# Grouped quads of a graph layer: sorting the edges' inputs instead of their messages

## The chip, the cores and the metric

One core of one Trainium2 chip. The metric is the device time of one execution, in microseconds (us). Three runs of the kernel before gave 2073.61, 2068.15 and 2074.27 us, median 2073.61. The profiled execution took 2069.4 us, 2067.6 of them inside the profiler's span.

## The reference, cut to what matters

200,000 edges, 6,250 nodes, 128 features. The kernel must compute

```
h    = relu(layernorm(x))                     # 6250 x 128
xw   = h @ W_in
W_e  = (softplus(f_e @ W_f1 + b_f1) - log 2) @ W_f2 + b_f2     # per edge, f_e has 20 numbers
m_e  = xw[dst_e] * W_e * c_e                  # the message of an edge
out  = segment_sum(m_e, src_e, 6250)
y    = x + (softplus(out @ W_o1 + b_o1) - log 2) @ W_o2 + b_o2
```

The edges come sorted by `dst`, so the gather `xw[dst]` of a run of edges touches a narrow window of nodes; `src` is random, so the segment sum is a scatter.

## The kernel before, in words

The edges are cut into chunks of 128, four chunks to a *quad* (512 edges, 391 quads). One pass of a long loop (line 1208) carries every quad through a software pipeline written out by hand: what runs in iteration i at which point ("L", "D0", "PE2", "A0", ...) is put into a table of hooks by `at(...)`, and each engine executes its instructions in that program order.

Every quad goes through the same message part. TensorE makes `z` from the filter inputs (`s1_pe`, L313; the 20 inputs are held as three bfloat16 parts in 123 rows of `ft`), ScalarE makes `a` from it (exp and ln, L318 and L323), TensorE makes `W` (a bias matmul L494 and four fp32 matmuls L505) and gathers the node rows `xg` with a one-hot of `dst` relative to a 21-node window (L497), ScalarE scales `xg` by the edge weight (`xc`, L510), and VectorE multiplies `W` by `xc` (L520): the messages. What becomes of them depends on the kind of quad.

- **Plain** quads (31, at the beginning and the end): equal `src` within a chunk are summed with a comparison matrix `eq` (L357) and a matmul (L532); then GpSimd scatters each chunk with one indirect, accumulating DMA (`scatter`, L582) into one of four accumulators in DRAM. Four scatters a quad.
- **Listed** quads (192): lists made beforehand (`l_eq`, `l_count`, ..., L366 to L444) send repeated nodes to rows of their own, so that the messages are scattered as they stand. Four scatters a quad, and one more per 16 quads for the list.
- **Sorted** (grouped) quads (168, in 21 rounds of 8): no scatter. The nodes are split into 16 groups of 392; every edge gets a slot among 16 x 32 slots by its group and its rank in it, and 64 overflow slots (`rank_group` to `rank_slot`). `perm_oh` (L662) makes the one-hot of slots, `part_rem` (L676) splits the messages into three bfloat16 parts, `permute` (L687) carries the parts into slot order on TensorE (16 matmuls a quad), `perm_out` (L693) copies them to bfloat16, and once in a round four *units* (`unit_oh` L766, `unit_pe` L781 with 96 matmuls, `unit_evac` L792) add the 8 quads' slots into `accT` in SBUF, four groups at a time. The overflow slots of two quads are moved by `over_pe` (12 matmuls, L702 to L704), summed (L718 to L755) and scattered with one scatter.

So the number of scatters is fixed by the kinds: the trace has 768 of listed quads, 123 of plain ones and 96 from overflow slots and lists. `sorted_quads` takes quad 8 and then steps of 2, 2, 2, 3 through the quads. After the loop come a check of flags, the sum of the accumulators and the output matmuls (L1353 to L1446).

The DMAs of the loop are issued by SP in program order: `load_sc` (L288) for a pair of quads brings `ft`, the relative `dst` (`rb`) and the window rows (`wn`); the three bfloat16 parts of the filter inputs are made in blocks of 8 quads (`fb_1` to `fb_4`, L268 to L286) and pass through DRAM (`fsd`). The program issues the scatters as

```
scatter(st[q]["m"][:, c, :P], lst["ji", w][:, 4 * k + c:4 * k + c + 1], l_base(w) + P)   # L803, per chunk
nc.gpsimd.indirect_dma_start(out=accs[k][:rows, :], out_offset=..., in_=s, compute_op=ALU.add)   # L582
```

and the two matmul groups that the change replaces are

```
for c in range(4):                                   # permute, L687; s = 0..3, so 16 a quad
    nc.tensor.matmul(t[:, :PW], mp[q]["pm"][:, c, s * P:(s + 1) * P], high(mp[q]["pt"][:, c:c + 1, :PW])[:, 0], ...)
for c in range(4):                                   # over_pe, L702 to L704; 12 a quad
    nc.tensor.matmul(o[:, :P + 3], w, pt[:, 2 * P:PW], ...)
    nc.tensor.matmul(o[:, :P], w, pt[:, P:2 * P], ...)
    nc.tensor.matmul(o[:, :P], w, pt[:, :P], ...)
```

Of the kernel before, what the change touches and what calls it, by code (L numbers as in the profile page):

```python
# [27 lines left out]
MP0 = 8  # L28
MPGAPS = (2, 2, 2, 3)
MPEND = 0  # L30
RND = 8
EXTRA = 0
RKQ = 8
UOFF = (2, 6)
SW = 16
LEARLY = 8
LLATE = 16
LCAP = 7
PW = 387
MW = 388  # L40
# [7 lines left out]
FPARTS = ((0, 3), (3, 2), (5, 1))  # L48
CQ = 16
EARLY_N = 256  # L50
ZMAX = 60.0
# [3 lines left out]
def tile_gnn(ctx: ExitStack, tc: tile.TileContext, x, fB, cT, srcT, srcr, dstr, win_, wf1, wf2, bias, bo1c, wo1,  # L55
             wo2, consts, ident, cmap, out, n_edges):
# [3 lines left out]
    NB, RB, BE = fB.shape  # L60
    EP = NB * BE
# [3 lines left out]
    NSC = EP // SC  # L65
    HALF = NSC // 2
    spread = big(NSC)
# [6 lines left out]
    caps = base_caps(NP, NSC)  # L74
# [3 lines left out]
    ZL = 3  # L78
    K1_END, K2_END, K3_END = 2, 8, 140
    Z2, Z3 = [0,0,1,1,2,2,3,3,4,4], [5+2*j for j in range(10)]  # L80
    mpq = sorted_quads(NQ)
    mpi = {q: n for n, q in enumerate(mpq)}
    units = unit_its(mpq)
    splain = [q for q in range(NQ) if q not in mpi]
    plain = {q: n for n, q in enumerate(splain)}
    NS = len(splain)
    LB, LE = listed(NS) if spread else (0, 0)
    CE = min(128, EP // P) if spread else EP // P
    CB = min(4 * NS + 64, EP // P) if spread else 0
    lend = splain[LE - 1] if LE else 0  # L90
    scat = [0] * (NQ + 60)
    for q in splain:
        scat[q + (2 if LB <= plain[q] < LE else 4)] += min(4, NCH - 4 * q)
    NW = (LE - LB) // SW
    LR = P * NW
    wend = [splain[LB + SW * (w + 1) - 1] for w in range(NW)]
    for w in range(NW):
        scat[wend[w] + 16] += 1
    for q in mpq[1::2] + mpq[-1:] * (len(mpq) % 2):
        scat[q + 10] += 1  # L100
# [8 lines left out]
    sp_ = edge.enter_context(tc.tile_pool(name="sp", bufs=4))  # L109
# [13 lines left out]
    fmax = cp.tile([P, NB], F32, name="fmax")  # L123
    zcol = cp.tile([P, 4], F32, name="zcol")
    loads = {}
# [3 lines left out]
    x_sb = cp.tile([P, NPT, P], F32, name="x_sb")  # L129
# [10 lines left out]
    accT = cp.tile([P, NP], F32, name="accT")  # L140
    zero = accT[:, :ACC_R // ZR]
    wgtb = cp.tile([P, 1], BF16, name="wgtb")
    iotw = cp.tile([P, GN // 2 + SLOTS], F16, name="iot")
    iot = iotw[:, GN // 2:]
    tri = cp.tile([P, P], BF16, name="tri")
# [3 lines left out]
    ge = cp.tile([P, 4 * RKQ, GRP + 1], BF16, name="ge")  # L149
    dropT = cp.tile([P, EP // P], BF16, name="dropT")  # L150
    mos = []
    for i in range(2):
        mo_ = cp.tile([P, 132], F32, name=f"mo{i}")
        mos.append(mo_)

# [14 lines left out]
    def zero_list(k, j):  # L170
        v = accs[k][ACC_R:].rearrange("(p t) f -> p (t f)", p=P)
        w = LR // ZL
        nc.sync.dma_start(v[:, j * w:(j + 1) * w], zero[:, :w])

    def xt_load(g):
        o, T = groups[g]
        nc.sync.dma_start(x_sb[:, o // P:o // P + T], x[o:o + T * P, :].rearrange("(t p) f -> p t f", p=P))
# [3 lines left out]
    def prep_stat(g):  # L181
# [3 lines left out]
        for t in range(T):  # L185
            nc.vector.bn_stats(bn[:, t], x_sb[:, o // P + t])
# [4 lines left out]
        pst[g] = {"mv": mv, "var": var}  # L191
# [8 lines left out]
    def prep_norm(g):  # L200
# [8 lines left out]
        for t in range(T):  # L209
            nc.vector.tensor_scalar(xn[:, t], x_sb[:, o // P + t], pst[g]["mv"][:, t, 0:1], rs[:, t:t + 1],  # L210
                                    op0=ALU.subtract, op1=ALU.mult)
# [51 lines left out]
    def fb_load(b):  # L263
        t_ = ld.tile([P, FE], F32, tag="fb", name="fb", bufs=2)
        nc.sync.dma_start(t_, fB[b].rearrange("r e -> (r e)").rearrange("(p e) -> p e", p=P))
        fst[b] = {"f": t_}
# [21 lines left out]
    def load_sc(s):  # L288
        n = min(SC, NQ * SEG - s * SC)
        pp, hh, nh = s % HALF, s // HALF, n // SEG  # L290
        top = caps[s]
        ft = fts[s % len(fts)]
        b, o = s * SC // BE, s * SC % BE
# [4 lines left out]
        for j in range(nh):  # L298
            nc.sync.dma_start(rb[j * HB:(j + 1) * HB], reld[s:s + 1, j * SEG:(j + 1) * SEG].to_broadcast([HB, SEG]))
        wn = ld.tile([P, 2, P], BF16, tag="wn", name="wn")  # L300
        _, regs = nc.values_load_multi_w_load_instructions(
            base_i[pp:pp + 1, hh, 0:2 * nh], engines=[SP], min_val=0, max_val=top,
            skip_runtime_bounds_check_because="clamped on the chip to [0, top]")
        for k in range(2 * nh):
            j, c = divmod(k, 2)
            nc.sync.dma_start(wn[j * HB:j * HB + NR, c, :], tab[bass.ds(regs[k] * 3, NR), :])
        loads[s] = (ft, rb, wn)

    def s1_pe(q):
        ft = loads[q // 2][0]  # L310
        j = q % 2
        z = ps.tile([P, 512], F32, tag="A", name="z", bufs=4)
        nc.tensor.matmul(z, ws, ft[:K1, j * SEG:(j + 1) * SEG], start=True, stop=True)  # L313
        st.setdefault(q, {})["z"] = z
# [10 lines left out]
    def s1_oh(q):  # L325
        if q % 2 == 0:
            rb = loads[q // 2][1]
            oh = wk.tile([P, 512], BF16, tag="oh", name="oh")
            v = slice(0, min(2, NQ - q) * HB)
            nc.vector.tensor_scalar(oh[v], rb[v], rowid[v], None, op0=ALU.is_equal)  # L330
            late["oh"] = oh
        st[q]["oh"] = late["oh"]
# [3 lines left out]
    def sb_load(k):  # L336
        qs = splain[2 * k:2 * k + 2]
        t_ = ld.tile([P, 2 * SEG], I16, tag="sb", name="sb", bufs=4)
        for j, q in enumerate(qs):
            if j and q == qs[0] + 1 and q % 2:  # L340
                continue
            n = 2 if j == 0 and len(qs) > 1 and qs[1] == q + 1 and q % 2 == 0 else 1
            o = q % 2 * SEG
            nc.sync.dma_start(t_[:, j * SEG:(j + n) * SEG],
                              src16[q // 2:q // 2 + 1, o:o + n * SEG].to_broadcast([P, n * SEG]))
        sbs[k] = t_

    def plainq(q):
        return q not in mpi and not LB <= plain[q] < LE

    def s1_eq(q):
        if not plainq(q):
            return
        n = plain[q]
        eq = wk.tile([P, 4, P], F32, tag="eq", name="eq", bufs=3)
        v = sbs[n // 2][:, n % 2 * SEG:(n % 2 + 1) * SEG]
        nc.vector.tensor_tensor(eq, v.rearrange("p (c i) -> p c i", c=4),  # L357
                                srcT_sb[:, n * 4:n * 4 + 4].unsqueeze(2).to_broadcast([P, 4, P]), op=ALU.is_equal)
        st[q]["eq"] = eq
# [13 lines left out]
    def l_count(g):  # L373
        t = ps.tile([P, 512], F32, tag="B", name="lcnt", bufs=4)
        for k in range(2):
            eq = lst.pop(("eq", 2 * g + k))
            for c in range(8):
                nc.tensor.matmul(t[:, 8 * k + c:8 * k + c + 1], eq[:, c, :], wgtb, start=True, stop=True)
        lst["cnt", g] = t
# [73 lines left out]
    def l_start(j):  # L453
        mp["L", j] = {"so": idl[:, j:j + 1]}

    def l_dg(j):
        dg = wk.tile([P, P], F32, tag="h", name="ldg", bufs=1)
        nc.scalar.mul(dg, idt, idl[:, j:j + 1])
        mp["L", j]["dg"] = dg

    def l_same(j):
        eq = wk.tile([P, P], F32, tag="rm", name="leq", bufs=1)
        nc.vector.tensor_scalar(eq, mp["L", j].pop("row")[:, :P], idl[:, j:j + 1], None, op0=ALU.is_equal)
        mp["L", j]["eq"] = eq

    def l_sum(j):
        t = ps.tile([P, 512], F32, tag="B", name="lsum", bufs=4)
        for k in range(NACC):
            nc.tensor.matmul(t[:, :P], mp["L", j]["eq"], lst["m", j][:, k], start=(k == 0), stop=(k == NACC - 1))
# [1126 lines left out]
```

## Time and profile before

| | us |
|---|---|
| median of three runs | 2073.61 |
| profiled execution | 2069.4 |
| its span | 2067.6 |
| PE busy (matmul) | 1854.7 |
| DVE busy | 1657.1 |
| POOL busy | 1631.5 |
| ACT busy | 1490.1 |

PE is TensorE, DVE VectorE, ACT ScalarE, POOL GpSimd, SP the engine that issues the plain DMAs. A group of instructions is shown as: line, engine, operation, output<-inputs, shapes, count, then busy time and mean ns of one, then the idle time of the engine just before them and what ended it. "issue" is idle time in which the engine waited for nothing that the profile shows. The busy times of groups add up to more than an engine's busy time, because the records of neighbouring instructions overlap: the DVE groups add up to 1828 us against 1657.1 of busy time. The granted TensorE clock was 0.96 over the span and 0.99 from 400 to 1900 us.

### The profile page before, as it was taken

Reading aid. Unit: us, or ns where it says so; the run is one execution under the profiler, and the core shown is the slowest. Engines: PE = TensorE matmul, PEld = TensorE weight load, DVE = VectorE, ACT = ScalarE, POOL = GpSimd, SP = SyncE. Lnnn points to the kernel's source line nnn. Section 1 sums busy time; section 2 is a strip of 40 time slices with the busy share of each in tenths; the row PEclk is TensorE's granted clock in tenths of the full one; section 3 lists DMA queues with packets and bytes.
Section 4 is the critical chain, followed back from the end, with each engine's and each line's share of the span. In section 5 each row is a group of like instructions: output and inputs, shape, how many; then the busy total and the mean of one; then the engine's idle time right before and its main releaser. Section 6 shows DMA issues by size and latency. Waiting matters only on the chain. (4 is left out here: it accounts for less than half of the span.)

```text
span 2067.6 us, 57535 instructions
## 1 busy us (share of the span) xinstructions
PE 1854.7 (90%) x20381; PEld 1285.7 (62%) x20381; DVE 1657.1 (80%) x4448; ACT 1490.1 (72%) x4083; POOL 1631.5 (79%) x1040
## 2 busy tenths in 40 slices
PE   3489997999999999999999999999999999999956
PEld 2356664666666666666666666666666666677734
DVE  3578896898987888988988978979889787787735
ACT  3368775777776788777778777777778678888714
POOL 3578888888877788887878878888888888888774
PEclk9689998999999999999999999999999999999978
DMA  7887766767766776766667666676676676667648
GB/s 240 227 211 150 125 124 109 128 112 135 130 124 106 126 133 117 136 124 122 121 133 123 122 123 117 118 129 107 129 128 116 112 126 111 110 120 131 129 46 242
DMA packets 381187, 272.56 MB, mean 132 GB/s; under 512 B 97727, under 2 KB 341354, under 8 KB 380898
## 3 DMA queue, kind: packets, MB, share of 16 engines
q0 software_dynamic: 143728, 71.30, 34.9%
q1 hardware_dynamic: 236882, 197.50, 33.8%
q8 instruction: 161, 2.64, 0.5%
q14 instruction: 128, 1.05, 0.2%
q10 hardware_dynamic: 288, 0.07, 0.0%
HBM read 154.45 MB, written 114.24 MB: 130 GB/s over the span
## 5 line engine op out<-in xcount | busy, mean ns | idle before, releaser
L582 POOL DMA_INDIRECT acc<-s,lji x768 | 1237.3, 1611 | 266.9 <-issue 184.6
L687 PE MATMUL pq<-pt,pm 128*128 128x387 bf16 x2688 | 527.9, 339 | 27.0 <-DVE pt L676 10.7
L510 ACT ACTIVATE xc<-xg,cb 128x128 f32<-128x128 f32 x1564 | 446.4, 371 | 121.0 <-PE xg L497 113.8
L505 PE MATMUL W<-w,a 128*128 128x128 f32 x3128 | 464.1, 293 | 0.0
L505 PEld LDWEIGHTS W<-w,a 128*128 128x128 f32 x3128 | 388.7, 196 | 42.0 <-issue 2.6
L781 PE MATMUL un<-so,mst 32*128 32x392 bf16 x8064 | 378.3, 331 | 31.9 <-ACT os L746 19.3
L693 ACT CAST mst<-pq 128x387 bf16<-128x387 f32 x672 | 303.1, 481 | 132.6 <-PE pq L687 130.0
L687 PEld LDWEIGHTS <-pm 128*128 128x128 bf16 x2688 | 259.4, 99 | 211.4 <-issue 16.7
L781 PEld LDWEIGHTS <-mst 32*128 32x128 bf16 x8064 | 228.4, 94 | 175.0 <-issue 70.0
L323 ACT ACTIVATE a<-a,con 128x512 f32<-128x512 f32 x391 | 282.3, 722 | 12.7
L582 POOL DMA_INDIRECT acc<-s,ji x123 | 197.0, 1602 | 82.8 <-issue 25.9
L318 ACT ACTIVATE a<-z 128x512 f32<-128x512 f32 x391 | 237.4, 607 | 33.2 <-PE z L313 17.4
L676 DVE TENSOR_TENSOR pt<-pt 128x512 f32<-128x512 f32 x336 | 231.8, 690 | 5.8
L662 DVE TENSOR_SCALAR pm<-iot,pos 128x576 bf16<-128x576 f16 x672 | 221.4, 390 | 0.0
L520 DVE TENSOR_TENSOR s<-W,xc 128x512 f32<-128x512 f32 x192 | 131.9, 687 | 92.9 <-ACT xc L510 86.0
L792 DVE TENSOR_TENSOR accT<-un,accT 128x392 f32<-128x392 f32 x320 | 158.5, 558 | 58.4 <-PE un L781 58.2
L766 DVE TENSOR_SCALAR so<-iot,mst 128x392 bf16<-128x392 f16 x672 | 191.2, 344 | 5.5 <-PE un L781 5.4
L582 POOL DMA_INDIRECT acc<-os,oji x96 | 155.6, 1621 | 31.1 <-issue 16.2
L497 PE MATMUL xg<-wn,oh 63*128 63x128 bf16 x1564 | 157.2, 222 | 14.5 <-ACT xc L510 8.1
L313 PE MATMUL z<-ft,ws 123*128 123x512 bf16 x391 | 151.6, 388 | 16.1 <-POOL b2rep L927 9.3
L494 PE MATMUL W<-b2rep,onesb 64*128 64x512 bf16 x391 | 153.8, 393 | 0.0
L520 DVE TENSOR_TENSOR pt<-W,xc 128x512 f32<-128x512 f32 x168 | 115.2, 686 | 34.9 <-ACT xc L510 29.4
(209 smaller groups left out, 2431.1 us busy)
## 6 DMA issues: line engine op xcount, KB each, us to landing
rb<-reld SPq DMA_DIRECT2D x391, 64.0 KB
fsd<-f SPq DMA_DIRECT2D x49, 480.0 KB
ft<-fsd SPq DMA_DIRECT2D x195, 120.0 KB
sb<-src SPq DMA_DIRECT2D x169, 128.0 KB
fb<-in_fB_dram SPq DMA_DIRECT2D x49, 320.0 KB
ft<-fsd SPq DMA_DIRECT2D x195, 80.0 KB
wn<-tab SPq DMA_DIRECT2D x782, 15.8 KB
acc<-s,lji POOLq DMA_INDIRECT x768
```

The lines of the kernel that those rows point to most:

```text
L318: nc.scalar.activation(a, st[q]["z"], AF.Exp)
L323: nc.scalar.activation(a, a, AF.Ln, bias=half, scale=0.5)
L505: nc.tensor.matmul(W[:, c, :], st[q]["a"][:, c * P:(c + 1) * P], w2, start=False, stop=(c == 3))
L510: nc.scalar.mul(xc[:, c, :], st[q]["xg"][:, c, :], late["c", q // CQ][:, 4 * (q % CQ) + c:4 * (q % CQ) + c + 1])
L520: nc.vector.tensor_tensor(m[:, :, :P], st[q]["W"], st[q]["xc"], op=ALU.mult)
L582: nc.gpsimd.indirect_dma_start(out=accs[k][:rows, :], out_offset=bass.IndirectOffsetOnAxis(ap=ji, axis=0), in_=s, in_offset=None, compute_ ...
L662: nc.vector.tensor_scalar(pm[:, c], iot[:, :SLOTS], rk[r]["pos"][:, 4 * j + c:4 * j + c + 1], None, op0=ALU.is_equal)
L676: nc.vector.tensor_tensor(pt[:, :, k * P:(k + 1) * P], a, high(a), op=ALU.subtract)
L687: nc.tensor.matmul(t[:, :PW], mp[q]["pm"][:, c, s * P:(s + 1) * P], high(mp[q]["pt"][:, c:c + 1, :PW])[:, 0], start=(c == 0), stop=(c == 3))
L693: nc.scalar.copy(mp[q]["ms", s][:, :PW], mp[q].pop(("q", s))[:, :PW])
L766: nc.vector.tensor_scalar(so, iotw[:, :GN], w[:, 3 * P // 2:3 * P // 2 + 1], None, op0=ALU.is_equal)
L781: nc.tensor.matmul(ts[g][:, :GN], mp[q]["ms", s][v, k * P:(k + 1) * P], mp[q]["oh"][v], start=(q == qs[0] and k == 0), stop=(q == qs[-1] a ...
```

## The change

The loop runs over a list of *items* instead of quads (class `Plan`): S for the quads that are scattered, B for grouped quads, V for an extra quad per round. Quad 12 and then every second quad to quad 378 is grouped (184 quads, 23 rounds of 8); 176 quads are listed, 31 plain; with 23 V items that makes 414 items. What the change does to a grouped quad:

- **Inputs are sorted, not messages.** For a round of 8 quads the filter inputs and the edge weight are loaded in edge order, 128 edges to the partitions (`nat_load`), split into three bfloat16 parts on ACT and DVE (`nat_1` to `nat_4`), and put beside a one-hot of the window (2 x 21 columns, `nat_win`) and the two numbers of the node: 108 columns an edge. `permute` carries these columns into slot order, as rows: 4 matmuls of 512 slots and 4 of the 64 overflow slots a quad, in place of 16 and 12.
- **Messages are made in slot order.** `z` comes from three matmuls with the rows of the three parts, the node rows from 12 matmuls with the sorted one-hot (`edge_win`), the weight and the node of a slot from four small matmuls (`b_ext`). The rest of the message part is as before; the messages stay in fp32 (`bms`).
- **The split in bfloat16 parts moves to the units**: `unit_parts` does it on 8 x 128 columns per unit; `unit_oh`, `unit_pe`, `unit_evac` are as before, now with the strided high halves of fp32 as weights.
- **Overflow slots of 8 quads form item V**: its 512 slots go through the message part and then the path of a plain quad, with `vrow` in place of the loaded `src` row; four scatters a round. `over_pe` to `over_scatter` go.
- The loads of filter inputs and the passes through DRAM (`fb_*`, `fsd`, `ft`, `rb`) are made for the S quads only; `x` is not kept in SBUF, but loaded again for the last addition: 8 of its 13 tiles near the end of the loop, 5 after it.
- Window rows of a grouped quad are loaded by `load_win` (2 loads of 21 nodes a quad). The pool of message buffers `s` has 5 in place of 4 buffers, `pm` has 1 in place of 2.

```diff
-MP0 = 8
-MPGAPS = (2, 2, 2, 3)
+MP0 = 12
+MPGAPS = (2,)
...
+    def load_win(q):
+        wn = wk.tile([P, 3, P], BF16, tag="wb", name="wb", bufs=pl.nwin)
+        for h, reg in enumerate(bases(q)):
+            o = KZ + h * WIN
+            nc.sync.dma_start(wn[o:o + WIN], tab[bass.ds(reg * 3, NR), :].rearrange("(r k) f -> r k f", k=3))
...
+    def rows3(z, ft):
+        for k, n in enumerate(ZROWS):
+            yield nc.tensor.matmul(z, wsb[:n, k], ft[:n], start=(k == 0), stop=(k == 2))
+
+    def edge_win(xg, ft, wn, c, k):
+        nc.tensor.matmul(xg[:, c, :], ft[KZ:KX, c * P:(c + 1) * P], wn[KZ:KX, k, :], start=(k == 0), stop=(k == 2))
...
+            cs = [(c, k) for c in range(4) for k in range(3)]
+            for j, _ in enumerate(rows3(z, ft)):
+                for c, k in cs[4 * j:4 * j + 4]:
+                    edge_win(xg, ft, bq[q]["wn"], c, k)
...
+        elif kind == "V":
+            for j, e in enumerate(pl.rounds[q]):
+                o = j % 2 * OVC
+                for k in range(3):
+                    nc.tensor.matmul(xg[o:o + OVC, j // 2, :], vq[q]["f"][KZ:KX, j * OVC:(j + 1) * OVC],
+                                     bq[e]["wn"][KZ:KX, k, :], start=(k == 0), stop=(k == 2))
...
+    def nat_load(r):
...
+            nc.sync.dma_start(fn[:, v] if n > 1 else fn[:, j], cols(fN, 4 * KN, q, d, n))
+            nc.sync.dma_start(dn[:, v] if n > 1 else dn[:, j], cols(dstT, 4, q, d, n))
+            for k in range(2):
+                nc.sync.dma_start(bn_[:, k, v] if n > 1 else bn_[:, k, j],
+                                  cols(base0[k:k + 1].to_broadcast([P, base0.shape[1]]), 2, q, d, n))
...
-    def permute(q, s):
-        t = ps.tile([P, 512], F32, tag="B", name="pq", bufs=4)
-        for c in range(4):
-            nc.tensor.matmul(t[:, :PW], mp[q]["pm"][:, c, s * P:(s + 1) * P], high(mp[q]["pt"][:, c:c + 1, :PW])[:, 0],
-                             start=(c == 0), stop=(c == 3))
+    def permute(q):
...
+        for c in range(4):
+            w = sts[r % 2][:, 4 * j + c, :]
+            nc.tensor.matmul(f[:KS], w, pm[:, c, :GRP * CAP], start=(c == 0), stop=(c == 3))
+            nc.tensor.matmul(o[:KS, :OVC], w, pm[:, c, GRP * CAP:], start=(c == 0), stop=(c == 3))
...
+    def slot_ext(t, f):
+        for c in range(4):
+            nc.tensor.matmul(t[:, 3 * c:3 * c + 3], f[:KS, c * P:(c + 1) * P], selb[:KS], start=True, stop=True)
...
+    def unit_parts(r, s):
+        m = bms[r % 2][:, :, s]
+        rm = wk.tile([P, RND, P], F32, tag="rem", name="rem", bufs=1)
+        nc.vector.tensor_tensor(rm, m, high(m), op=ALU.subtract)
+        lo = wk.tile([P, RND, P], BF16, tag="low", name="low", bufs=1)
+        nc.vector.tensor_tensor(lo, rm, high(rm), op=ALU.subtract)
...
+            at(max(0, i - 3), "L", nat_load, r)
...
+                at(max(0, u - WLEAD + 4), "L", load_win, q)
+                at(u - 1, "D2", perm_oh, q)
+                at(u, "PE2", permute, q)
+                at(u + 1, "A0", perm_out, q)
+                at(pl.ext[q], "PE2", b_ext, q)
+                at(pl.ext[q] + 1, "D0", b_ext_copy, q)
+                at(p, "A0", b_copy, p)
```

Here `u` is the item in which a grouped quad is sorted, at most 7 items before its own place `p`, and `i` the item in which its round is ranked.

1102 lines of the change are left out of this document (610 added, 492 removed).

## The prediction

> **What bounds the kernel now.** I read the busy times first. PE is busiest, so it looks like the bound; three engines lie close behind.
>
> ```profile
> PE 1854.7 (90%) x20381; PEld 1285.7 (62%) x20381; DVE 1657.1 (80%) x4448; ACT 1490.1 (72%) x4083; POOL 1631.5 (79%) x1040
> ```
>
> Then the costliest groups. Three of them are one instruction, the scatter: 768 + 123 + 96 = 987 on POOL.
>
> ```profile
> L582 POOL DMA_INDIRECT acc<-s,lji x768 | 1237.3, 1611 | 266.9 <-issue 184.6
> L582 POOL DMA_INDIRECT acc<-s,ji x123 | 197.0, 1602 | 82.8 <-issue 25.9
> L582 POOL DMA_INDIRECT acc<-os,oji x96 | 155.6, 1621 | 31.1 <-issue 16.2
> ```
>
> Third, POOL's timeline in the middle of the run. The columns are start, duration, engine, line; the bracket is the idle time before.
>
> ```profile
> 1000.56 1.54 POOL L582 DMA_INDIRECT acc<-s,lji  x1 [0.30 <-issue]
> 1002.40 1.54 POOL L582 DMA_INDIRECT acc<-s,lji  x1 [0.30 <-issue]
> 1004.25 1.56 POOL L582 DMA_INDIRECT acc<-s,lji  x1 [0.31 <-issue]
> ```
>
> The reader is to see that 0.30 us follow every scatter although nothing is waited for: "79% busy" is a full engine. A scatter costs 1589.9/987 = 1.611 us plus 0.306 (226.7 us of "issue" before 742 of them), 1.917 in all. The table by stretches gives the middle:
>
> ```profile
> 400.00:1900.00 1500.00, 1429.70 (x16202) 985.08 (x16201) 1272.82 (x3442) 1155.26 (x3181) 1236.17 (x766) 0.99 0.69 122
> ```
>
> The columns after the stretch are the busy times of PE, PEld, DVE, ACT and POOL, then the clock, the DMA share and GB/s. POOL made 766 scatters in 1500 us, 1.958 each: 98% of its full rate. PE was busy 95%, DVE 85%. At the end POOL runs alone, with PE at 1.2 of 12 us from 1996 to 2008; its last scatter is
>
> ```profile
> 2006.32 1.54 POOL L582 DMA_INDIRECT acc<-os,oji  x1 [0.30 <-issue]
> ```
>
> So **POOL's queue of scatters is the bound**, with PE level beside it. The execution as a sum: first scatter at 55.2; 987 x 1.917 = 1892; POOL waits for others 60; 59.7 from the last scatter's end (2007.9) to 2067.6. The run itself is 1.8 us longer than the span (2069.4), and the median of the runs is 1.002 times that.
>
> **The change part by part, POOL.** Listed quads fall from 192 to 176 and plain ones stay at 31; a round still sends four overflow scatters (before one per two quads, now item V), and there are 23 rounds for 21. The instruction lists show 704 + 215 + 11 = 930 scatters, 57 fewer: 57 x 1.917 = **-109 us**. Two memsets of 3456 columns join POOL's start; by the 32x1024 row (946 ns) they take 6.4 us, beside 9.8 us in which POOL waited for `b2p`. I count 3 us (0 to 6.4). After the loop 1.09 MB of `x` are loaded again; from 2015 us the tail moved 242 GB/s at a DMA share of 0.89, so +4.5 us (0 if the loads hide).
>
> **PE.** Marginal prices come from starts in PE's timeline, since the records overlap:
>
> ```profile
> 1003.67 1.56 PE L687 MATMUL pq<-pt,pm 128*128 128x387 bf16 x8
> 1005.16 0.25 PE L702 MATMUL po<-pt,pm 128*64 128x131 bf16 x1
> 1005.99 0.39 PE L494 MATMUL W<-b2rep,onesb 64*128 64x512 bf16 x1
> 1006.32 1.16 PE L505 MATMUL W<-w,a 128*128 128x128 f32 x8
> 1007.31 0.38 PE L313 MATMUL z<-ft,ws 123*128 123x512 bf16 x1
> 1007.62 4.16 PE L781 MATMUL un<-so,mst 32*128 32x392 bf16 x96
> 1011.72 0.39 PE L494 MATMUL W<-b2rep,onesb 64*128 64x512 bf16 x1
> ```
>
> Eight `pq` take 1.49 (0.187 each), twelve `po` 0.83, a bias matmul with four `xg` 0.33, W 0.99 to 1.09, a unit 4.10. Removed: 168 quads x (16 x 0.187 + 0.83) = 642; overflow sums 84 x 0.58 (`orow` 0.30, `osum` 0.28) = 49; per grouped quad the 123-row `z` (0.22) and the `xg` (0.11), 61. Added: `permute`, four times a 512-column matmul (0.22, the `z` row) and a 64-column one (0.06, the `po` spacing), 184 x 1.12 = 206; `z` and windows, three 512-column matmuls each beside four of 128 on other rows. The nearest row is bias beside `xg`, 0.33, so 184 x 0.99 = 182 (0.66 if fully concurrent, 1.3 if not: 121 to 239). `b_ext` by `lcnt` (16 in 0.40): 21. Eight more units 33. Per V item 0.66 + 0.22 + 24 x 0.06 + 1.09 + 1.4 (eight fp32 records and the four weight sums) + 0.3 = 5.1, x 23 = 117. The weight column of plain quads as its own matmul: 15. Net 574 - 752 = -178: PE 1855 -> **about 1677** (1616 to 1734).
>
> **DVE.** Removed: `part_rem` 231.8; overflow instructions 59.5; 23 of 49 input blocks at 2.45, 56; 92 `oh` at 0.36, 33; 8 `eql` 10; together 390. Added: `unit_parts` 184 x 1.22, the 128x1024 `eql` row, 224, so that the split costs nearly what it did; 64 more `pm` and `so` 39; 32 evacuations 16; 23 message products 16; 184 small PSUM copies at 0.22 (the `ldup` row) 41; `nat_*` 23 x 4.2 (three passes priced by the 128x640 rows, 0.82; two one-hots at most the 512 row, 0.68; two small ones) 97; V 30; two rounds of ranking 10. Sum 473. Net +83; the groups add up to 1828 for 1657 busy, so x 0.906 = +75: DVE 1657 -> **about 1732**. ACT loses 519 us by the rows (303 of `mst`, 183 of `pt` columns and overflow work, 33 of input blocks) and gains about 268 (154 for sorted columns, 57 for 23 items, 57 other); it ends near 1240 and binds nothing.
>
> **DMA and SP.** Each round adds 128 x 8 x 4 = 4096 packets, some of 8 and 16 bytes, 94,000 in all; about 50,000 go (`ft`, `rb`, `wn`, `fsd`, `fb`). The plain queue spends 0.338 x 16 x 2067.6 / 236,882 = 47 ns a packet, so the share of 0.69 rises by some 0.04 (by 0.1 if a tiny packet costs twice that). SP issues fewer DMAs but reads bases 391 times instead of 196; a pair's window loads start about 1.1 us after its other loads in the trace, so +0.2 ms of SP time, in a queue whose longest wait (278 us behind `f`, L284) falls by half. I cost both at nothing; what hides them is the lead of the loads, below.
>
> **The sum.** 2067.6 - 109 + 3 + 4.5 = 1966 span, with POOL's 60 us of waits kept. That is the choice: DVE has less spare, but `s` has five buffers and PE is 10% lighter. Plus 1.8, times 1.002: **1972**. If the 60 us vanish 1912; if scatters also ran at 1.54, 1846.
>
> A rule that speaks against it: scatters of 1.54 us in the quiet end average 1.61 in the run. The Trainium skill ("SBUF — State Buffer", "SBUF: two separate sides") says that VectorE's two-port instructions lock GpSimd out of a shared port pair, so that it cannot write descriptors. The trace agrees in the direction, but no row ties a long scatter to one DVE instruction; by the rule the sum would be that of the second rival.
>
> **Rivals.**
> - *DVE takes over.* Needed in the middle: 23 rounds of 36.5 scatters at 1.917 are 70 us each, and DVE's share of a round is about 66 (1732, less an estimated 210 of work at both ends, by 23). Its waits speak for it:
>
> ```profile
> DVE s L520 <- ACT xc L510: 86.0, 85, 4.2
> DVE accT L792 <- PE un L781: 58.2, 54, 5.3
> DVE ojd L751 <- ACT os L746: 49.5, 21, 13.7
> ```
>
> The third goes with the overflow path; the second stays; of all `xc` waits (132) I keep half. 1732 + idle at the start 33, from 60 to 200 us 40, from 1960 on 58, + 58 + 66 = 1987, so 1993. With `pm` single, `perm_oh` waits for `permute` where two quads are sorted in consecutive items (45 times, at most 2 us): up to 2083.
> - *Scatters stretch.* The 0.07 us above 1.54 grows with DVE's busy share (80% to 88%): 930 x 0.007 = 7 us, 1979.
> - *Late loads, slower than before.* Place: `nat_load` in SP's queue. Its 4096 packets fill each of 16 engines for 12 us at 47 ns, 24 at twice that. `load_pair` behind it is issued three items before use, some 13.5 us. At 24 us it comes about 14.6 us late (4 of its own included); with one quad buffered for POOL (7.7) the starved rest is 6.9 x 23 rounds = 159: 2131. It is slower than before from about 4.4 us of starvation a round. Against it: PE waited 6.0 us for `ft` in the whole run, and the burst shares the engines with little else.
> - *POOL better fed* than now, below 1940.
> - That overflow falls into the slow repair loop I exclude: counted on the reference's inputs, a quad overflows by at most 57 of its 64 slots.
>
> **How the numbers follow.** 1972 as the bound stays POOL: 0.50 (1940 to 1995). DVE 0.25 (1993 to 2060, a tenth of it beyond). Stretch 0.05. Late loads 0.11. Better fed 0.09. The range from 1925 to 2060 leaves out half of the last and nearly all of the slow cases. Faster by over 0.3%, about what a measurement of this kernel tells from none: 0.86; within it 0.03; slower 0.11.
>
> **What would show it.** Right: 930 scatters with 0.30 us before nearly each, PE near 1680, DVE near 1730, a last scatter near 1903 and 64 us behind it. DVE as bound: POOL's idle before scatters released by DVE `s`, DVE over 92% in the middle. Late loads: PE `z` or `xg` waiting for DMA `ft`, `wn` or `wb` once per 17 items. Wrong altogether if strided weights slow the units (4.10 us) or the scatter's price moves.

## The result, and the profile after

The changed kernel takes 2409.73 us (median of 4 runs, 2405.53 to 2415.01) where the kernel before takes 2072.39 beside it (2068.15 to 2074.27): a ratio of **1.163, interval 1.160 to 1.167**. The forecast was 1972 us with a range to 2060. It is wrong in sign and lies 438 us too low. The profiled execution took 2406.4 us, with a span of 2404.6.

The busy times of the changed kernel:

```profile
PE 1975.6 (82%) x21648; PEld 1389.7 (58%) x21648; DVE 1717.5 (71%) x4480; ACT 1257.1 (52%) x3311; POOL 1583.2 (66%) x988
```

DVE (1732 forecast) and ACT (1240) came out as worked out. PE should have been 1677. Every share is lower than before, while the run is longer. The scatters in the groups of the changed kernel (count, busy, mean ns, idle time before them and what ended it):

```profile
L672 POOL DMA_INDIRECT acc<-s,lji x704 | 1166.5, 1657 | 498.7 <-DVE s L604 174.0 <-issue 165.3 <-DMA acc<-s,lji 91.4
L672 POOL DMA_INDIRECT acc<-s,ji x215 | 350.0, 1628 | 258.2 <-ACT ji L653 160.0 <-issue 48.3 <-DMA acc<-s,ji 40.2
L672 POOL DMA_INDIRECT acc<-os,oji x11 | 17.3, 1577 | 5.1 <-ACT oji L541 2.4 <-ACT a L362 1.5 <-issue 0.9
```

The count is the 930 of the forecast and the price nearly so (1.649 us in the mean, 1.611 before). But POOL now waits for others: 762 us of idle before scatters, of which "issue" is only 214. Its timeline at the place shown of before, and its last scatter:

```profile
1003.39 1.81 POOL L672 DMA_INDIRECT acc<-s,ji  x1 [8.16 <-ACT r L208]
1005.50 1.54 POOL L672 DMA_INDIRECT acc<-s,ji  x1 [0.30 <-issue]
...
2336.00 1.54 POOL L672 DMA_INDIRECT acc<-s,ji  x1 [0.30 <-issue]
```

The first scatter starts at 75.5 us (55.2 before), the last one ends at 2337.5. With 930 x 1.917 taken off, the time between them leaves 479 us in which POOL waits for others, where the prediction kept 60. The 67 us behind the last scatter are near the 64 of the forecast.

The table by stretches of the changed kernel (PE, PEld, DVE, ACT, POOL, then granted clock, DMA share and GB/s):

```profile
400.00:1900.00 1500.00, 1283.60 (x14748) 885.19 (x14747) 1141.55 (x3027) 820.57 (x2175) 989.30 (x597) 0.89 0.49 81
```

In the same 1500 us the kernel before made 766 scatters with PE 1429.70, at a clock of 0.99 and a DMA share of 0.69. Now it makes 597, one each 2.51 us, PE is busy 86% at a clock of 0.89, and the DMA engines have *less* to do. What the clock is about shows in PE's timeline:

```profile
1007.95 0.19 PE L809 MATMUL po<-pm,st 128*108 128x64 bf16 x1
1009.01 0.63 PE L536 MATMUL lrw<-ldg,onesf 128*128 128x128 f32 x2 [0.87 <-ACT xc L594]
1009.57 0.60 PE L560 MATMUL W<-b2rep,onesb 64*128 64x512 bf16 x1
...
1010.11 2.07 PE L577 MATMUL W<-w,a 128*128 128x128 f32 x8
...
1012.85 1.14 PE L518 MATMUL lsum<-lm,leq 128*128 128x128 f32 x8
...
1014.35 1.16 PE L577 MATMUL W<-w,a 128*128 128x128 f32 x8
```

After a stop of 0.87 us eight fp32 matmuls take 2.07 us. At 1012.85 eight of the same shape take 1.14 again, and so do the next ones of this line (1.16). The granted clock of the single microseconds from 1009 to 1013 is 0.61, 0.50, 0.50 and 0.68, so it was half for about 3.4 us. A PE that has waited works more slowly for some microseconds here, and its "busy" time grows without more work.

To separate the two, I weighted PE's busy time with the granted clock in steps of 2 us. Before: 1854.7 us busy are 1811 at full clock, with 213 us of idle beside them. After: 1975.6 are 1747, with 428 idle. The 337 us between the spans are therefore **-64 of work, +185 of slow clock, +215 of idle time**.

What ended the idle times of DVE and of PE in the changed kernel (us in all, times, longest):

```profile
DVE s L604 <- ACT xc L586: 180.6, 126, 11.3
DVE accT L893 <- PE un L882: 116.5, 57, 5.1
DVE eql L418 <- DMA sb<-src: 100.9, 12, 13.6
```

```profile
PE xg L565 <- DVE oh L378: 84.8, 51, 4.0
PE be L823 <- DVE ex L832: 43.0, 4, 12.3
PE po L809 <- DVE ex L832: 33.6, 9, 5.0
```

DVE waits for loads, for ACT and for PE; PE waits for small things that DVE owes (a one-hot, a copy of 12 columns). Two places show how. First, a round's loads, in SP's timeline:

```profile
438.48 0.41 SPq L687 DMA_DIRECT2D fn<-in_fN_dram  x1
438.94 0.57 SPq L688 DMA_DIRECT2D dn<-in_dstT_dram  x1
439.56 1.95 SPq L690 DMA_DIRECT2D bn<-in_base_dram  x2
441.55 10.62 SPq L388 DMA_DIRECT2D sb<-src  x4
```

`nat_load` issues 4096 packets of 8 to 336 bytes. Behind it four `sb` issues take 10.62 us; the median of one is 0.43. Everything stops for it, DVE first, then PE:

```profile
456.96 1.22 DVE L418 TENSOR_TENSOR eql<-sb,srcT_sb 128x1024 bf16<-128x1024 int16 x1 [13.57 <-DMA sb<-src]
```

```profile
459.01 0.77 PE L536 MATMUL lrw<-ldg,onesf 128*128 128x128 f32 x2 [14.10 <-DVE ex L832]
```

Such stops come about a round apart: DVE waits 8 to 14 us for `sb` at 257, 358, 457, 1110, 1210 and 1314 us, and about 3 us at 733, 826 and 919. Second, DVE's order, in its timeline and in PE's:

```profile
1016.36 0.85 DVE L698 TENSOR_REDUCE fmax<-fn 128x1 f32<-128x672 f32 x1
1017.12 1.22 DVE L860 TENSOR_TENSOR rem<-bm 128x1024 f32<-128x1024 f32 x1
1018.37 1.23 DVE L862 TENSOR_TENSOR low<-rem 128x1024 bf16<-128x1024 f32 x1
1019.52 1.01 DVE L869 TENSOR_SCALAR so<-iot,ex 128x392 bf16<-128x392 f16 x4
1020.44 0.16 DVE L832 COPY ex<-be 128x12 f32<-128x12 f32 x1
```

```profile
1017.18 0.38 PE L808 MATMUL pf<-pm,st 128*108 128x512 bf16 x1
1020.65 0.21 PE L809 MATMUL po<-pm,st 128*108 128x64 bf16 x1 [3.09 <-DVE ex L832]
```

PE wants a PSUM bank for `po`. By the order of the program the bank is free when DVE has copied the 12 columns of `be`, and that copy of 0.16 us stands at the head of the next item, behind all that DVE has to do for this one: ranking, splitting, one-hots.

### The profile page after: what moved, and what is told of

It reads as the page before. It is cut to its first block, busy times and chain, and to the rows that moved or that the text cites. A ratio compares the mean times of both kernels' runs of the same rounds, so it can differ in the third digit from the quotient of the medians.

```text
span 2404.6 us, 58531 instructions
## 1 busy us (share of the span) xinstructions
PE 1975.6 (82%) x21648; PEld 1389.7 (58%) x21648; DVE 1717.5 (71%) x4480; ACT 1257.1 (52%) x3311; POOL 1583.2 (66%) x988
## 3 DMA queue, kind: packets, MB, share of 16 engines
q1 hardware_dynamic: 283038, 153.25, 24.1%
## 5 line engine op out<-in xcount | busy, mean ns | idle before, releaser
L672 POOL DMA_INDIRECT acc<-s,ji x215 | 350.0, 1628 | 258.2 <-ACT ji L653 160.0
L882 PE MATMUL un<-so,bm 32*128 32x392 bf16 x2944 | 342.8, 359 | 12.4 <-DVE ldup L434 5.6
L882 PE MATMUL un<-so,rem 32*128 32x392 bf16 x2944 | 330.1, 357 | 0.0
L882 PE MATMUL un<-so,low 32*128 32x392 bf16 x2944 | 326.1, 352 | 0.0
L586 ACT ACTIVATE xc<-xg,cb 128x128 f32<-128x128 f32 x828 | 239.5, 386 | 95.3 <-PE xg L565 44.2
L808 PE MATMUL pf<-pm,st 128*108 128x512 bf16 x736 | 244.2, 423 | 6.4 <-ACT s L627 3.9
L594 ACT ACTIVATE xc<-xgb,ex 128x128 f32<-128x128 f32 x736 | 207.3, 363 | 0.0
L869 DVE TENSOR_SCALAR so<-iot,ex 128x392 bf16<-128x392 f16 x736 | 193.7, 325 | 0.0
L339 PE MATMUL xgb<-wb,bfe 42*128 42x128 bf16 x2208 | 190.5, 221 | 3.5 <-DVE accT L893 3.5
L336 PE MATMUL z<-bfe,wsb 64*128 64x512 bf16 x552 | 178.4, 392 | 0.2
```

What stands on the lines that cost most here:

```text
L336: yield nc.tensor.matmul(z, wsb[:n, k], ft[:n], start=(k == 0), stop=(k == 2))
L339: nc.tensor.matmul(xg[:, c, :], ft[KZ:KX, c * P:(c + 1) * P], wn[KZ:KX, k, :], start=(k == 0), stop=(k == 2))
L586: nc.scalar.mul(xc[:, c, :], st[n]["xg"][:, c, :], v)
L594: nc.scalar.mul(xc[:, c, :], xg[:, c, :], bq[q]["ex"][:, c, 0:1])
L808: nc.tensor.matmul(f[:KS], w, pm[:, c, :GRP * CAP], start=(c == 0), stop=(c == 3))
L869: nc.vector.tensor_scalar(so, iotw[:, :GN], bq[q]["ex"][:, s, 1:2], None, op0=ALU.is_equal)
```

## The experiments

Four theories were tried. **A**: late loads (`nat_load`), the prediction's slower rival. **B**: hand-overs between PE and DVE, through banks and through the order on DVE. **C**: DVE's amount of work. **D**: PE's own work. Beside them stands the prediction's first step: POOL's queue as the bound of the kernel before. All ratios are to the kernel before, run on the same chip as the experiment. Differences between ratios are given in us of its median, 2072. Runs without an interval were single runs; the others have two or more.

### Round loads packed (e1)

```diff
-        for j, dj, q, d, n in runs(pl.rounds[r]):
-            ... fn, dn, bn_ from columns of fN, dstT, base0 (strided by quad)
+        nc.sync.dma_start(fn, fR[:, RND * 4 * KN * r:RND * 4 * KN * (r + 1)])
+        nc.sync.dma_start(dn, dstT[:, RND * 4 * r:RND * 4 * (r + 1)])
+        nc.sync.dma_start(bn_, base0[r:r + 1].to_broadcast([P, 4 * RND]))
```

> The changed kernel with the loads of a round (node-ordered features, target indices, window bases) laid out by rounds, so that one round is 3 DMAs of 128 packets instead of 4 DMAs of 7168 small ones; the same work otherwise. Theory A (late loads: the small packets hold SP's queue, and four sb issues behind them took 10.6 us at 441.6 instead of 1.7): DVE's waits for sb fall from 101 to under 25 us, the four or five PE pauses of 12 to 14 us a hundred us apart go, and the time falls by 100 to 170 us, to about 2240 to 2310. Theory B (the lock-step through the PSUM banks and DVE's order makes the loss; loads only show up where there is slack): under 40 us, 2370 to 2410. If it is all late loads, as the prediction's slower rival had it, the time comes down to about 1990.

Measured: 2337.3 us, ratio 1.120 (1.118 to 1.123), **89 us faster** than the changed kernel; clock 0.885. (The 7168 in the text above is a slip: the packets fell by 3728 a round, so there were about 4096.) DVE's wait before `eql`:

```profile
DVE eql L418 <- DMA sb<-src: 14.2, 6, 7.7
```

SP's timeline now shows four `sb` issues right behind the round's loads at their usual price:

```profile
325.79 1.86 SPq L388 DMA_DIRECT2D sb<-src  x4
```

Theory A's waits went as it said, from 101 to 14 us; the gain of 89 us is about as large as they were and lies a little below its range of 100 to 170. Four fifths of the 438 us over the forecast stay.

### The two small edits for the banks, each alone (e2, e3)

```diff
-        nc.vector.tensor_copy(ex..., bq[q].pop("te")[:, :12])      # b_ext_copy, at ext + 1, "D0"
+        nc.scalar.copy(ex..., bq[q].pop("te")[:, :12])             # e2: at ext + 1, "A0"
```

```diff
-            xg = ps.tile([P, 4, P], F32, tag="B", name="xgb", bufs=4)
+            xg = ps.tile([P, 4, P], F32, tag="A", name="xgb", bufs=4)   # e3
```

> The changed kernel with the small copy of `be` (128x12) made by ScalarE one item after its matmul instead of VectorE. Theory B (PE waits for the bank that this copy frees, and it stands in DVE's queue behind the long work of the item before): the PE waits be, po, rkp and lrw released by DVE ex (122 us in all) go nearly to zero, the clock rises, and the time falls by 60 to 150 us. Theory A (late loads): those waits were only the echo of DVE being held by sb; 0 to 40 us. Theory C (DVE itself is late, whatever it frees): the waits come back under another name (oh, accT, G), the time moves by less than 30 us.

> The changed kernel with the four sums of windows (`xgb`) in the other group of four PSUM banks, that of z, xg and W, so that the group B holds one bank less. Theory B (too few banks in group B): waits released by ACT xc L594 (lcnt, rkp, lpre: about 30 us) go, POOL's and ACT's idle falls, 40 to 120 us faster. Theory A and C: within 25 us of the changed kernel; or a few tens slower, where z now waits for a bank of group A.

Measured, one run each: e2 2430.7 us, ratio 1.164, nothing gained; e3 2401.3, ratio 1.150, 28 us. In e2 PE's waits for `ex` on DVE are gone, and others took their place:

```profile
PE lcnt L428 <- ACT xc L594: 45.1, 10, 6.6
PE W L560 <- DVE bm L604: 43.7, 4, 14.3
```

The second has the length of a stop for `sb`. It seems that as long as DVE is held by loads, it does not matter which of its debts PE runs into. Taken alone this spoke for A and C against B.

### The kernel before without 192 scatters (e4)

```diff
             for c in range(nchunks(q)):
+                if c == 3:
+                    sc_n[0] += 1
+                    continue
                 scatter(st[q]["m"][:, c, :P], ...)                  # listed quads
```

> The kernel before, with the fourth of the four scatters of each listed quad left out (192 of 987; those edges' sums are missing from the output). The prediction's first step says that POOL's queue is the bound: POOL then needs 795 x 1.917 = 1524 us, and PE, level beside it, is left as the bound: the time falls to where PE is busy throughout, about 1970 to 2010. If POOL was not the bound but PE (95% busy, 99% from 1700 to 1900): within 20 us of the kernel before, 2050 to 2075.

Measured, one run: 2054.2 us, ratio 0.983, 34 us. POOL had 192 x 1.917 = 368 us less to do.

```profile
400.00:1900.00 1500.00, 1426.40 (x16231) 984.59 (x16231) 1268.43 (x3448) 1153.11 (x3191) 982.75 (x602) 1.00 0.61 115
```

PE, DVE and ACT do in these 1500 us what they did before (1429.70, 1272.82, 1155.26); POOL is at 66% instead of 82%, and the pace is nearly the same (about 1% higher by the ratio, because this chip runs the kernel before in 2089 us). The 34 us are a little more than the 20 that the second expectation allowed, and far from the 1970 to 2010 of the first. **POOL's queue was full, but it was not the bound.**

### The order of `oh`, DVE's amount, PE's amount, POOL's amount (e5 to e8, all on e1)

```diff
-            if i < NI:
-                s1_oh(i)
+            if i + 1 < NI:
+                s1_oh(i + 1)                                        # e5
```

```diff
-        ... rm and lo: two passes of 128x1024 over the messages     # e6, unit_parts
-        un[r, s] = (high(m), high(rm), lo), []
+        un[r, s] = (high(m),) * 3, []
```

```diff
-            for k in range(3):                                      # e7, unit_pe
+            for k in range(2):
```

In e6 the units add the first part three times in place of the three parts, so PE's work stays. e8 has e4's edit in the changed kernel.

> The kernel with packed round loads (e1, 1.120 of before) and with the one-hot `oh` of a plain or listed quad's targets made one item earlier, ahead of VectorE's other work of the item. Same work. Theory B2 (what is left is the lock-step: PE stops 53 times, 100 us, for `oh`, which stands behind the long stretch of VectorE's item before; each stop lowers the granted clock): these waits go below 30 us, the clock rises from 0.885, 50 to 120 us faster, ratio 1.06 to 1.10. Theory C (VectorE is late whatever it hands over): the waits come back at the next thing that it owes, s or bm, G, pm or ex; less than 30 us, ratio 1.105 to 1.125.

> The kernel with packed round loads (e1) and without the split of the collected messages into three parts: the two passes of `unit_parts` are left out, 184 of 1.22 us (224 us of VectorE's 1714), and the units read the first part three times, so the sums of grouped quads keep only the first of three parts. PE, ACT, POOL and the loads are unchanged. Theory C (VectorE's in-order queue is what PE waits for): 80 to 200 us faster, the clock above 0.92, ratio 1.03 to 1.08. Theory D (PE's own work at the granted clock is the bound, and VectorE has room): less than 30 us.

> The kernel with packed round loads (e1) and with two of the three parts in the units' matmuls (64 instead of 96 in each of 92 units; the third part is still computed and not added). PE loses 92 x 32 matmuls: by the 4.10 us of a unit 126 us at full clock. Theory D (PE is the bound): 110 to 160 us faster, ratio 1.045 to 1.07. Theory C (VectorE's order and the waits between the engines set the pace): under 60 us, ratio above 1.09, and PE's idle time grows by the rest.

> The kernel with packed round loads (e1) and without the fourth scatter of each listed quad (176 of 930; those edges' sums are missing from the output). The prediction's step (the sum is POOL's queue) would give 176 x 1.917 = 337 us less. Theories B, C and D: POOL is no bound, under 30 us; if the shorter queue frees message buffers earlier, up to 50.

| run | taken away | time, us | ratio (interval) | against e1 |
|---|---|---|---|---|
| e5 | nothing, `oh` one item earlier | 2260.8 | 1.089 (1.085 to 1.093) | -65 |
| e6 | 224 us of DVE | 2135.7 | 1.029 (1.026 to 1.032) | -190 |
| e7 | 126 us of PE | 2234.6 | 1.077 (1.071 to 1.082) | -91 |
| e8 | 337 us of POOL | 2321.3 | 1.118 (1.115 to 1.122) | -4 |

POOL counts for nothing. Of the time that the removed instructions cost, 0.85 comes back on DVE and 0.72 on PE. Counted by what the engines' busy time lost, it is nearly all: 199 us of DVE (1714 to 1515), and 95 us of PE at full clock (1755 to 1660, weighted as above). Two engines that worked side by side would not both give so much; I read it as their taking turns. In e5, with the same work, the waits that it was made for are gone. PE's row in e1, then in e5:

```profile
PE xg L565 <- DVE oh L378: 99.9, 53, 4.2
PE xg L565 <- DVE oh L378: 1.7, 1, 1.7
```

So a part is order (B2, the order of DVE's work). e6 fits C, but in it this row falls to 15.1 us too: the cut takes work from in front of `oh`, so that its 190 us hold some of what e5 gains by order alone. e7 lies between the forecasts of C and D in time, and PE's idle time did not grow (374.5 us in e1, 374.0 in e7), which speaks against C's reading of it.

### More hand-overs moved (e9, e10), and more work for PE (e11)

e9 is e5 with the edits of e2 and e3. e10 adds

```diff
-            at(k - 2, "D2", unit_parts, r, s)
+            at(k - 3 if r + 1 < len(pl.rounds) else k - 2, "D2", unit_parts, r, s)
```

and e11 is e5 with

```diff
-        nc.tensor.matmul(W..., onesb[b:b + HB], b2rep[b:b + HB]..., start=True, stop=False)
+        for h in range(3 + 1):
+            nc.tensor.matmul(W..., onesb[b:b + HB], b2rep[b:b + HB]..., start=True, stop=(h < 3))
```

> The kernel with packed round loads and the early `oh` (e5, 1.089 of before) and with both of the edits that were tried alone and gave 0 and 28 us: the small copy of `be` on ScalarE, `xgb` in the other group of banks. Same work. Theory B (each hand-over between PE and VectorE that is taken out gives its waits back once the larger ones are gone): the waits by ex (rkp 30, po 25, un 20) and by xc L594 go, 40 to 90 us faster, ratio 1.045 to 1.07. Theory C (VectorE is late by its amount of work): under 20 us.

> As e9, and the split of the messages (`unit_parts`, 2.44 us of VectorE ahead of each unit) one item earlier, so that an item's stretch of VectorE work at a unit is shorter by a third. The amount is the same. Theory B2 (bursts, not the amount, make VectorE late): another 20 to 60 us off e9. Theory C (the amount): within 15 us of e9.

> The kernel e5 (packed loads, early `oh`) with the bias matmul of W made four times instead of once for each of 414 items: 1242 more matmuls of 512 columns, by 0.22 us each 273 us of PE's time at full clock, output unchanged. Theory D (PE's own work is the bound): 200 to 280 us slower, ratio 1.185 to 1.225. Theory B (PE spends some 12% of its time stopped and some more at the half clock that follows a stop; the extra work is done partly in that time and keeps the clock up): 60 to 150 us slower, the clock rises above 0.93.

Measured: e9 2224.1 us, ratio 1.071 (1.065 to 1.078), 37 us less than e5, a little under what B expected. The two edits gave 0 and 28 us alone; with these intervals 37 cannot be told from their sum, so it isn't shown that they act more strongly together. e10 2185.0, ratio 1.053 (1.047 to 1.058), another 39 us without a change of amount. e11 2405.1, ratio 1.159 (1.152 to 1.165), 144 us *more* than e5 for 1242 more matmuls. Weighted with the clock PE's work is 1996 us in e11 against 1762 in e5, so 234 more (runs with the same matmuls spread from 1747 to 1764). Some 0.6 of each microsecond of PE is paid: more than nothing, and less than by a bound. The clock rose only from 0.909 to 0.920, so the filler did not buy it back.

### Where the ranking stands (e14, e18), and DVE's amount once more (e17, on e10)

```diff
-        self.rank = [self.perm[qs[0]] - 7 for qs in self.rounds]
+        self.rank = [self.perm[qs[0]] - 12 for qs in self.rounds]   # e14; 15 in e18
```

> As e10 (1.053 of before), and a round's ranking and its input split (rank_group, nat_max, nat_2, nat_4, nat_win, rank_own, rank_slot: about 10 us of VectorE over six items) five items earlier, so that it no longer falls on the item of the round's first unit. In e10 PE waited 28 us before units for `pr` and VectorE had up to 8 us of work in one item there; summed over the plan the work above 5.3 us in an item falls from 152 to 100 us. Theory B2 (bursts): 20 to 50 us faster, ratio 1.03 to 1.045. Theory C (amount): within 12 us of e10.

> As e14, but the ranking of a round begins eight items earlier than in e10 instead of five, so that both of its banks are free two items before the round's first unit. The work above 5.3 us in an item is 103 us by the plan (e14 100, e10 152). Theory B2 (order): the waits of PE before units for `pr` and `rt` (28 us in e10, 66 in e14) go, 40 to 80 us faster than e10 with the clock's part, ratio 1.015 to 1.035. Theory C (amount): within 12 us of e10 and e14, 1.045 to 1.055.

> As e10 (1.053 of before), without the split of the messages (the same cut as in e6: 224 us of VectorE, one part of three summed). In e1 that cut gave 190 us when VectorE's hand-overs were still late. Theory C (VectorE's amount still sets the pace with PE): 80 to 140 us, ratio 0.985 to 1.015. Theory B (the hand-overs that e5, e9 and e10 moved were what the cut had relieved): under 50 us, ratio above 1.03, and PE above 95% busy in the middle.

Measured: e14 2185.6 us, ratio 1.048 (1.043 to 1.054), and e18 2170.3, ratio 1.046 (1.044 to 1.049): 9 and 13 us by the ratios, and e14's interval overlaps that of e10. e17 2105.0, ratio 1.012 (1.010 to 1.015), 83 us for 224 us of DVE. PE's largest wait of this kind in e10, e14 and e18:

```profile
PE un L878 <- DVE pr L758: 28.2, 10, 4.0
```

```profile
PE un L878 <- DVE rt L782: 65.6, 21, 4.7
```

```profile
PE un L878 <- DVE ldup L434: 71.0, 22, 4.7
```

I read this as one wait under three names. A unit needs all four banks of its group, so it waits for whatever DVE frees last, and moving one debt away brings up the next. Theory C's expectation holds for e14 and e18 (within 12 us, or nearly), and e17's 83 us lie at the lower end of its range; the split's microsecond on DVE is worth 0.37 now instead of 0.85.

### What held the kernel before (e12, e13, e15, e16)

e12 has e7's edit in the kernel before (115 us of PE), e13 that and e4's. e15 leaves `part_rem` out, e16 has all three cuts.

```diff
     def part_rem(q, k):
         ...
-        nc.vector.tensor_tensor(pt[:, :, k * P:(k + 1) * P], a, high(a), op=ALU.subtract)
```

> The kernel before with two of the three parts in the units' matmuls (64 instead of 96 in each of 84 units): 2688 fewer matmuls, 84 x 1.37 = 115 us of PE by the 4.10 us of a unit. POOL, VectorE, ScalarE and the loads as before. If PE was the bound of the kernel before, as the run without 192 scatters suggests: 80 to 115 us faster, ratio 0.945 to 0.96. If POOL was, as the prediction's first step has it: under 20 us. If both stood level: about 30.

> The kernel before with both cuts: without the fourth scatter of each listed quad (192 of 987) and with two of three parts in the units (115 us of PE). Alone they gave 34 and 25 us. If POOL and PE stood level and each covered the other: more than the sum of both, 100 to 140 us, ratio 0.93 to 0.95. If neither was the bound, but the order between the engines (a third engine, VectorE at 85% in the middle): about the sum or less, 40 to 65 us, ratio 0.97 to 0.98, with the clock lower again.

> The kernel before without its split of the messages (`part_rem`, 336 of 0.690 us, 232 us of VectorE's 1657): the second and third parts are zeros that were written once, so the sums of sorted quads keep one part of three. PE, ACT, POOL and loads unchanged. If VectorE was the bound: 100 us or more, ratio under 0.955. If PE, POOL and VectorE stood level, each covering the others: 15 to 40 us, ratio 0.98 to 0.993, with POOL at 98% of its rate from 400 to 1900 us again. If VectorE had room: under 10 us.

> The kernel before with all three cuts: 192 scatters, a third of the units' matmuls and `part_rem` left out. The first two together gave 75 us (0.964). If VectorE was the third level engine: another 60 to 120 us, ratio 0.905 to 0.935. If it had room: 0.955 to 0.965.

| run | taken away | time, us | ratio (interval) | gain, us |
|---|---|---|---|---|
| e4 | 368 us of POOL | 2054.2 | 0.983 | 34 |
| e12 | 115 us of PE | 2051.0 | 0.988 (0.983 to 0.993) | 25 |
| e15 | 232 us of DVE | 2046.8 | 0.985 (0.980 to 0.990) | 32 |
| e13 | POOL and PE | 2009.9 | 0.964 (0.958 to 0.970) | 75 |
| e16 | all three | 1966.0 | 0.946 (0.943 to 0.948) | 113 |

e4 is a single run, and the intervals of e12 and e15 reach some 10 us to either side. The first two alone make 59, all three alone 91; together they make 75 and 113, which with these intervals is hardly more than the sums. So none of the three was the bound. Of what is taken away from one engine alone 9% (POOL), 22% (PE) and 14% (DVE) comes back. e12 and e15 alone came out as engines that stand level would have it (about 30; 15 to 40). The joint cuts gave less than such engines should: e13's 75 lies between its two expectations (40 to 65, 100 to 140), and so do e16's 38 us for its third cut.

In e12 the stretch from 400 to 1900 us reads

```profile
400.00:1900.00 1500.00, 1384.03 (x14203) 944.27 (x14201) 1285.31 (x3486) 1172.24 (x3230) 1254.26 (x775) 0.97 0.70 124
```

775 scatters instead of 766: POOL, at 99% of its rate, lets little more through, and PE, with less to do, stands still more and loses clock (0.99 to 0.97). Relieving one engine runs into the others. Whether it is their amounts or the order between them isn't settled for the kernel before.

## Why the prediction was wrong, point by point

- **The failed step: "So POOL's queue of scatters is the bound, with PE level beside it"**, and the sum built on it, with 57 x 1.917 = 109 us taken off at full price and "POOL's 60 us of waits kept". The reading of POOL was right (0.30 us after every scatter, 98% of its rate). The conclusion was not: a queue that is full need not set the pace if others are nearly full too. By e4 a microsecond of POOL was worth 0.09, so I estimate 10 us for the 57 scatters. And the waits were not kept: by the prediction's own count they are 479 us in place of 60. e8 shows the same in the changed kernel: 176 scatters fewer gave 4 us.
- **What set the pace** in its place, beside the late loads (89 us), was PE and DVE waiting for each other. The forecast costed each engine by its sum of work and let them run beside each other. In the changed kernel they take turns (0.85 and 0.72 in e6 and e7): earlier hand-overs with the same work gave 153 us in all (e5 to e18). Each turn leaves a gap on PE, and slow clock follows the gaps. Between the two spans lie 337 us: 215 more of idle PE and 185 of slow clock, against 64 of work saved. The prediction had no term for either.
- **"PE 1855 -> about 1677"** was mis-sized: -64 us at full clock, not -178. From starts in PE's timeline, weighted with the clock, summed over the run: `z` and windows of grouped quads 217 us (182 forecast; 1.18 a quad, between 0.99 and the upper bound of 1.3), `permute` 219 (206), and bias matmuls with `xg`, without the `xg` of item V, 151. The last were 130 before and I let them fall by 20: the bias matmul had been hidden beside its quad's `xg` (0.33 for both), and a grouped quad has none at that place any more, so it costs 0.32 alone. These three are +35, +13 and +41, 89 of the missing 114. The units were right: 385.7/92 = 4.19 us, 362.6/84 = 4.32 before, so strided weights cost nothing.
- **DVE 1732, ACT 1240, 930 scatters** were right (1717, 1257, 930), and useless without the order. The rival "DVE takes over" named the right engine, but not how: its sign was DVE over 92% in the middle, and DVE is at 76%. It added DVE's busy time and half of its own waits; what PE loses by waiting for DVE was not in it, and 2083 was its end. `pm` with one buffer cost DVE 25 us, against at most 90.
- **"Scatters stretch"** had the sign right and the size too small: 1.611 to 1.649 us a scatter, 0.038 where it expected 0.007, some 35 us of POOL's time, which by e8 cost next to nothing.
- **"Late loads"** was right in place (`nat_load`, 4096 packets, once per round) and too large in size (159 us worked out, 89 measured), and got 0.11. It named the wrong victim, `load_pair` behind it; what came late was `sb`, which SP issued late. The price was wrong as well: a packet of the plain queue took 33 ns in the mean (0.241 x 16 x 2404.6 / 283,038), not 47.
- **"I cost both at nothing"** for DMA share and SP: the share fell (0.69 to 0.49) where it was to rise by 0.04, and SP's part was not free, as e1 shows.

Against the kernel before the loss is 16.3% of its time. Packed loads give back 4.3, the earlier `oh` 3.1, `ex` and `xgb` together 1.8, the earlier `unit_parts` 1.9, the ranking 0.6; **4.6 stay** in e18, the fastest version with all of the work. No version with the whole computation beats the kernel before. Leaving the split out still gives 83 us for 224 of DVE (e17). That cut takes away amount and, with it, the stretch of work ahead of each unit, and no run separates the two. Whether another order of the same work could give the rest back isn't settled, since each move so far brought up the next wait. That the stops cause the slow clock is a reading of the timeline; no run changed the clock by itself.

An estimate of what the idea could give at best: PE's 1747 us at full clock with the overhead of the kernel before (2067.6/1811 = 1.142) are 1995, 3.5% less than before.

## What to carry to other kernels

An engine that is full in the profile is a candidate for the bound, and one cheap cut of its work shows whether it is one. Here, with three engines at 85 to 98%, a cut on one of them was worth a tenth to a fifth of its price. In the changed kernel, where none is full, a cut on PE or DVE was worth 0.7 to 0.85 of it. When a change rewrites the order of work, cost the hand-overs and not only the sums: for each small result that another engine needs, ask what stands ahead of it in its engine's queue, and which bank it holds meanwhile. Many small descriptors held up the queue that issues them, so lay data out by use before it is loaded.

## What the runs showed of the hardware

- **Issuing can stall behind earlier small packets.** Four `sb` issues took 10.62 us behind `nat_load`, and meanwhile the 16 DMA engines had little to do on average (a mean does not show whether one of them was full). The table by stretches of the changed kernel has a DMA share of 0.11, and 5 GB/s, for five of these microseconds:

```profile
445.00:450.00 5.00, 0.00 (x0) 0.00 (x0) 0.00 (x0) 1.96 (x6) 2.59 (x2) 0.60 0.11 5
```

  From 443 to 449 us the trace has 635 packets, all of 8 bytes, about 105 a microsecond. By their size they are the window bases (`bn`), the smallest packets of the round's loads. e1 packed all three kinds of loads at once and doesn't separate them. With 384 packets a round instead of 4096, four such issues took 1.86 us. The Trainium skill ("DMA: Bandwidth & Descriptors", "Issuing engines are not separate DMA queues") calls the sequencer's time to start a DMA usually small; here it was 10.62 us ahead of a wait of 13.57.
- **Half clock followed a stop of under a microsecond.** After 0.87 us of idle the granted clock was half from 1009.2 to 1012.6. The Trainium skill ("TensorE: Matmul & The Clock Gate", "What's actually happening") gives about 3.4 us, of idling to lose the clock and of work to regain it, in windows that run freely; the trace agrees in the length of the slow stretch and shows it after a shorter stop.
- **Scatters were shorter without the split on DVE.** Without the split of the messages, which is DVE's work, the mean of a scatter fell from 1.644 to 1.595 us (e1 to e6), from 1.652 to 1.602 (e10 to e17) and from 1.611 to 1.588 (before to e15). Cuts of PE's work left it at 1.652 (e7) and 1.616 (e12). This is the direction of the rule that the prediction set against itself; no run shows by what mechanism.
- **A weight load of 108 columns** took 0.13 us in the changed kernel, one of 128 columns 0.09 to 0.10.
